# Joining layer norm statistics on GpSimd instead of VectorE in an eight-layer hybrid kernel

## The chip, the cores and the metric

The kernel runs on one core of a Trainium2 chip. The metric is the device time of one execution in microseconds. Before the change it is 443.06 us, the median of 5 runs (441.74 to 447.71). TensorE is called PE, VectorE DVE, ScalarE ACT, GpSimd POOL, and SyncE, which here only issues transfers, SP.

## The reference

The input `x` has 8 sequences of 256 tokens with 128 features, all in float32. Eight layers follow each other. Each reads a layer norm of `x` without weights, and its result is added back to `x`:

```python
x = L0_attn_a_x                      # (8, 256, 128)
x = x + causal_attention(layernorm(x))     # one head, softmax
x = x + ffn_relu(layernorm(x))             # expert 0 of a 128-512-128 network; ends in a layer norm of its own
x = x + linear_attention(layernorm(x))     # no softmax
x = x + ffn_relu(layernorm(x))             # same weights
x = x + retention(layernorm(x))            # 16 heads of 8, decaying causal mask
x = x + ffn_silu(layernorm(x))             # 128-384-128, integer weights times 1/127
x = x + softmax_attention(layernorm(x))    # 16 heads of 8, not causal
x = x + ffn_silu(layernorm(x))             # same weights

def layernorm(x, eps=1e-5):
    m = mean(x, -1); v = var(x, -1)
    return (x - m) / sqrt(v + eps)
```

So there are eight norms ahead of layers and two more inside the two `ffn_relu`.

## The kernel before, in words

The 2048 tokens are cut into four groups of 512 tokens, which are two sequences or four tiles of 128 tokens. A group's `x` stays in SBUF from start to end as a tile of 128 partitions by 4 by 128. Tokens lie on the partitions, so a layer norm's statistics run along the free dimension, one tile of 128x128 at a time.

Each group goes through the layers in order (`layers`, L1341), written as a generator. It asks for a step of an engine with an expected duration (`yield step(DVE, 0.4)`), for buffers (`get`), or for other threads to end (`join`), and then issues the instructions of the step. A planner (`Plan`, L136) runs the four generators and some threads for the weights against each other on a modelled clock while the program is built. Whenever an engine is free, the planner takes the waiting step with the lowest rank. The outcome is one fixed order of instructions on each engine; on the chip each engine then works its list off in that order and waits by semaphores where an operand isn't there.

What the order depends on is: the expected durations in the steps; `RANKS`, one number for each group and layer; `FIRST` and `LAST`, the ranks of the weights' threads; `STALL`, `LEEWAY` and `LATE`, which add to a step's rank or to a buffer's release time; and the times at which the weights' threads start (`plan.start(...)`, L1352 to L1360).

The change is in `layernorm` (L532). For each tile, DVE makes the statistics of the tile with `bn_stats` (L540), which writes six numbers: count, mean and sum of squared deviations of the even elements, and the same for the odd ones. Then DVE joins these to mean and variance with `bn_aggr` (L541). When all tiles are done, four small instructions follow for all tiles at once: variance plus epsilon (L547), minus the mean (L548), the power -1/2 (L551), and the product of minus the mean with it, called `shift` (L552). All four run on POOL. In a quick norm, which only the first layer uses, the first two run on DVE. In all there are 45 calls: 5 quick ones, 32 of four tiles and 8 of two tiles. The last come from the final `ffn_silu`, which works on one sequence at a time.

After that the tiles are normalised by ACT (L558, scale and bias) or DVE (L563, subtract and multiply), whichever the planner finds free. PE transposes them (L579) into PSUM, and ACT or DVE copies them out (L443).

Other names that matter here: in `ffn_relu` (L737) POOL adds the row `b2` to the normalised tiles (L745), `beta` to `x` (L610) and multiplies by `gamma` (L781) after the layer's own norm; its matmuls are L752 and L765. POOL also adds a row to `x` in retention and in softmax attention (L610), sums retention's states (L940) and may take part of its rotation (L831, L837). Preparing weights means the casts of the integer weights on DVE (L509, L510), retention's means (L498, L499) and small products. The softmax attention's scores are L1156, its maxima L1177 on DVE, its exponentials L1211 on ACT, its weighted sums L1228.

Of the kernel before, what the change touches and what calls it, by code (L numbers as in the profile page):

```python
# [30 lines left out]
ALU = mybir.AluOpType  # L31
# [3 lines left out]
B, S, D = 8, 256, 128  # L35
# [10 lines left out]
EPS = 1e-5  # L46
# [21 lines left out]
ARRIVALS = (3.1, 5.1, 6.8, 8.3)  # L68

PAGE, PAGE_US = 256, 3.7  # L70
STALL = 3.87
LEEWAY = 0.04


RANKS = [
    [-4.55, -2.84, -5.08, -11.21, -6.22, 0.79, -0.71, 3.83],
    [0.53, -0.33, -7.21, -3.58, 1.17, -5.41, 2.93, 4.66],
    [2.22, -0.01, -0.03, 8.64, 2.51, 3.26, 3.72, 4.3],
    [3.69, 1.03, 11.09, 5.47, 3.1, 3.24, -6.87, 4.5],
]  # L80
FIRST, LAST = -3.82, 0.45
LATE = 0.55


def of_act(n):
# [217 lines left out]
def step(engine, us, table=None, mode=None, n=None):  # L303

    return ("step", ((engine, us, table),), mode, int(us / 0.053) if n is None else n)
# [23 lines left out]
def hybrid(ctx: ExitStack, tc: tile.TileContext, t: dict, out: bass.AP):  # L329
    nc = tc.nc  # L330
    plan = Plan()
# [96 lines left out]
    def view(buf, pattern, n=N, **sizes):  # L428
        return buf[:, :n].rearrange(pattern, **sizes)

    def flat(tl):
        return tl.rearrange("p a b -> p (a b)")
# [13 lines left out]
    def constants():  # L446
        yield step(POOL, 1.2)
        for e in range(2):
            half = slice(64 * e, 64 * e + 64)
            nc.gpsimd.memset(chunk_mul[half, :], 1.0)  # L450
            nc.gpsimd.affine_select(
                out=chunk_mul[half, :], in_=chunk_mul[half, :], compare_op=ALU.is_ge,
                fill=0.0, base=0, pattern=[[1, 64]], channel_multiplier=-1,
            )
        for store in (r_values, r_spread, l_values, l_spread):
            for _, _, tl in list(store.items):
                if tl.shape[1] == 2:
                    yield step(ACT, of_act(576))
                    nc.scalar.copy(flat(tl), levels[:, 1:2].to_broadcast([P, 2 * tl.shape[2]]))
                else:  # L460
                    for c in range(2):
                        yield step(ACT, of_act(4 * S))
                        nc.scalar.copy(tl[:, :, c, :], levels[:, c : c + 1].unsqueeze(1).to_broadcast([P, 4, S]))
        made["constants"] = True
# [16 lines left out]
    def linear_weights():  # L481

        w = buffer("b_w", [P, P])
        ps = yield get(bank)
        yield step(PE, 0.25)
        nc.tensor.matmul(ps[:, :P], b_tp[:, 1, :], b_tp[:, 0, :], start=True, stop=True)
        yield step(DVE, 0.2)
        nc.vector.tensor_scalar_mul(w, ps[:, :P], float(D**-0.5))
        put(bank, ps)
        made["linear"] = w  # L490
# [41 lines left out]
    def layernorm(src, y, quick=False):  # L532
        s = yield get(small)
        nt = src.shape[1]
        stats = view(s, "p (t c) -> p t c", 6 * nt, t=nt)
        mv = s[:, 24 : 24 + 2 * nt].rearrange("p (t c) -> p t c", t=nt)
        rstd, shift = s[:, 32 : 32 + nt], s[:, 36 : 36 + nt]
        for i in range(nt):
            yield step(DVE, 0.4)
            nc.vector.bn_stats(stats[:, i, :], src[:, i, :])  # L540
            nc.vector.bn_aggr(mv[:, i, :], stats[:, i, :])  # L541
        if quick:
            yield step(DVE, 0.13)
        else:
            yield step(POOL, 1.14 + 0.16 * nt)
        e = nc.vector if quick else nc.gpsimd
        e.tensor_scalar(rstd, mv[:, :, 1], EPS, None, ALU.add)  # L547
        e.tensor_scalar(shift, mv[:, :, 0], -1.0, None, ALU.mult)  # L548
        if quick:
            yield step(POOL, 0.66 + 0.16 * nt)  # L550
        nc.gpsimd.tensor_tensor(rstd, rstd, minus_half[:, :nt], ALU.pow)  # L551
        nc.gpsimd.tensor_tensor(shift, shift, rstd, ALU.mult)  # L552

        def half(tiles):
            for i in tiles:
                e = yield either((ACT, 0.39), (DVE, 0.25), mode=PORT)
                if e == ACT:
                    nc.scalar.activation(  # L558
                        y[:, i, :], src[:, i, :], AF.Identity, bias=shift[:, i : i + 1],
                        scale=rstd[:, i : i + 1],  # L560
                    )
                else:
                    nc.vector.tensor_scalar(  # L563
                        y[:, i, :], src[:, i, :], mv[:, i, 0:1], rstd[:, i : i + 1],
                        ALU.subtract, ALU.mult,
                    )

        yield join([spawn(half(range(k * nt // 2, (k + 1) * nt // 2))) for k in range(2)])
        put(small, s)

# [781 lines left out]
    plan.start(causal_weights(), FIRST, 3.8)  # L1352
    for g in range(GROUPS):
        plan.start(layers(g), g, ARRIVALS[g])
    plan.start(constants(), LAST, 32.4)
    plan.start(linear_weights(), LAST, 15.4)
    plan.start(retention_weights(), LAST, 15.5)
    plan.start(silu_weights(), LAST, 23.7)
    plan.start(softmax_weights(), LAST, 45.7)
    plan.start(pairs_of_scores(), FIRST, 0.0)  # L1360
    plan.run()
    return plan
# [103 lines left out]
```

## Time and profile before

| what | value |
|---|---|
| median of 5 runs | 443.06 us |
| the profiled execution: time, span | 446.1 us, 444.4 us |
| mean granted clock of PE | 0.968 |
| busy: PE | 424.2 us (95%) |
| busy: DVE | 340.2 us (77%) |
| busy: ACT | 233.8 us (53%) |
| busy: POOL | 138.4 us (31%) |
| `bn_stats` on DVE | 160 times, 43.2 us |
| `bn_aggr` on DVE | 160 times, 29.1 us |
| the power on POOL | 45 times, 43.6 us |

A profile is one execution; its span runs from the first to the last instruction, and its time is a little longer than that. The busy shares are averages over stages that have different limits: the first 150 us hold the layers with many norms and small products, and the time from 184 to 398 us holds the softmax attention's scores beside everything else. The chain of waits is followed back from the last instruction; it says what a given stretch was waiting for.

### The profile page before, as it was taken

Reading aid. Unit: us, or ns where it says so; the run is one execution under the profiler, and the core shown is the slowest. Engines: PE = TensorE matmul, PEld = TensorE weight load, DVE = VectorE, ACT = ScalarE, POOL = GpSimd, SP = SyncE. Lnnn points to the kernel's source line nnn. Section 1 sums busy time; section 2 is a strip of 40 time slices with the busy share of each in tenths; the row PEclk is TensorE's granted clock in tenths of the full one; section 3 lists DMA queues with packets and bytes.
Section 4 is the critical chain, followed back from the end, with each engine's and each line's share of the span. In section 5 each row is a group of like instructions: output and inputs, shape, how many; then the busy total and the mean of one; then the engine's idle time right before and its main releaser. Section 6 shows DMA issues by size and latency. Waiting matters only on the chain.

```text
span 444.4 us, 12665 instructions
## 1 busy us (share of the span) xinstructions
PE 424.2 (95%) x5136; PEld 301.7 (68%) x5136; DVE 340.2 (77%) x990; ACT 233.8 (53%) x489; POOL 138.4 (31%) x244
## 2 busy tenths in 40 slices
PE   7899898999996999999999999999999999999996
PEld 6767686675875486767767557766666765674586
DVE  6978998877979879998789989857797615971353
ACT  3589845646152534234567734498416475245642
POOL 4145748859442643021231721301112000020020
PEclk9999999999959999999999999999999999957999
DMA  7300000003000301500001103000200011000001
GB/s 276 124 1 2 1 1 0 1 1 49 3 3 1 50 4 38 62 3 4 4 4 30 25 7 45 3 7 15 37 14 13 15 39 27 3 2 1 1 13 36
DMA packets 8041, 10.73 MB, mean 24 GB/s; under 512 B 1000, under 2 KB 6888, under 8 KB 7984
## 3 DMA queue, kind: packets, MB, share of 16 engines
q1 hardware_dynamic: 7904, 9.81, 9.8%
q8 instruction: 40, 0.66, 0.6%
q14 instruction: 17, 0.14, 0.1%
q10 hardware_dynamic: 80, 0.13, 0.1%
HBM read 4.43 MB, written 1.05 MB: 12 GB/s over the span
## 4 chain that ended last, share of the span: by engine, by line
PE 79%; DVE 13%; POOL 2%; ACT 2%; issue 2%; DMA 1%; DVEq 0%; ACTq 0%; POOLq 0%
PE bank L1156 19%; PE bank L1228 7%; PE bank L1086 5%; PE bank L752 5%; PE bank L1070 5%; PE bank L1076 5%; PE bank L970 4%; PE bank L896 4%; PE bank L765 4%; PE bank L579 2%; PE bank L620 2%; PE bank L817 2%; PE bank L931 2%; DVE small L540 2%; PE bank L1241 2%
## 5 line engine op out<-in xcount | busy, mean ns | idle before, releaser
L1177 DVE TENSOR_REDUCE small<-bank 128x2 f32<-128x512 f32 x128 | 80.4, 681 | 22.3 <-PE bank L1156 21.9
L1211 ACT ACTIVATE probs<-bank 128x512 f32<-128x512 f32 x128 | 68.0, 598 | 44.2 <-PE bank L1156 43.3
L1156 PE MATMUL bank<-l_spread 32*128 32x256 f32 x1024 | 90.8, 418 | 0.0
L547 POOL TENSOR_SCALAR small<-small 128x4 f32<-128x4 f32 (+1 forms) x40 | 11.0, 274 | 215.0 <-DVE small L541 209.9
L1156 PEld LDWEIGHTS bank<-l_spread 32*128 32x128 f32 x1024 | 58.2, 193 | 23.8 <-ACT probs L1211 5.7
L443 ACT COPY work<-bank 128x512 f32<-128x512 f32 (+3 forms) x76 | 35.8, 489 | 58.0 <-PE bank L579 15.3
L558 ACT ACTIVATE work<-x,small 128x128 f32<-128x128 f32 x79 | 34.5, 486 | 30.8 <-POOL small L552 30.8
L551 POOL TENSOR_TENSOR small<-small,mhalf 128x4 f32<-128x4 f32 (+1 forms) x45 | 43.6, 970 | 6.5 <-DVE small L548 6.5
L540 DVE BATCH_NORM_STATS2 small<-x 128x6 f32<-128x128 f32 x128 | 34.6, 270 | 3.6 <-DMA x<-in_x 3.3
L1228 PE MATMUL bank<-probs,l_values 128*32 128x256 f32 x512 | 35.0, 400 | 0.8 <-ACT small L443 0.7
L443 DVE COPY work<-bank 128x256 f32<-128x256 f32 (+3 forms) x36 | 19.0, 530 | 21.0 <-PE bank L1228 16.1
L541 DVE BATCH_NORM_AGGREGATE small<-small 128x2 f32<-128x6 f32 x160 | 29.1, 182 | 5.6
L765 PEld LDWEIGHTS bank<-c_relu,work 128*128 128x128 f32 x256 | 30.2, 192 | 3.2 <-issue 1.6
L765 PE MATMUL bank<-c_relu,work 128*128 128x128 f32 x256 | 32.1, 278 | 0.2 <-DVE work L757 0.2
L752 PE MATMUL bank<-work,c_relu 128*128 128x512 f32 x64 | 31.1, 603 | 1.2 <-ACT work L443 1.0
L579 PE MATMUL bank<-ident,work 128*128 128x128 f32 x128 | 22.8, 292 | 3.3 <-ACT work L558 1.8
L1228 PEld LDWEIGHTS bank<-probs,l_values 128*32 128x32 f32 x512 | 14.3, 112 | 16.6 <-issue 7.4
L1086 PE MATMUL bank<-c_ints,work 128*128 128x128 f32 x192 | 24.8, 279 | 0.0
L940 POOL TENSOR_TENSOR work<-work,work 128x272 f32<-128x272 f32 x16 | 13.0, 817 | 37.9 <-DVE work L918 37.8
L1086 PEld LDWEIGHTS bank<-c_ints,work 128*128 128x128 f32 x192 | 22.9, 192 | 2.6 <-issue 1.5
L1070 PE MATMUL bank<-work,c_ints 128*128 128x256 f32 (+1 forms) x72 | 24.3, 461 | 0.3 <-ACT work L443 0.2
L1076 PE MATMUL bank<-work,c_ints 128*128 128x256 f32 (+1 forms) x72 | 23.0, 453 | 0.0
(155 smaller groups left out, 758.7 us busy)
## 6 DMA issues: line engine op xcount, KB each, us to landing
r_spread<-wide SPq DMA_DIRECT2D x32, 64.0 KB
l_spread<-wide SPq DMA_DIRECT2D x32, 64.0 KB
out<-x SPq DMA_DIRECT2D x8, 128.0 KB
x<-in_x SPq DMA_DIRECT2D x3, 256.0 KB
c_retention_vo<-in_retention_vo SPq DMA_DIRECT2D x1, 713.0 KB
c_relu<-in_relu SPq DMA_DIRECT2D x1, 706.0 KB
c_retention_qk<-in_retention_qk SPq DMA_DIRECT2D x1, 641.0 KB
c_ints<-in_ints SPq DMA_DIRECT2D x1, 576.0 KB
```

Source lines behind the costliest of these rows:

```text
L443: (nc.scalar.copy if e == ACT else nc.vector.tensor_copy)(dst, src)
L540: nc.vector.bn_stats(stats[:, i, :], src[:, i, :])
L551: nc.gpsimd.tensor_tensor(rstd, rstd, minus_half[:, :nt], ALU.pow)
L752: nc.tensor.matmul(ps, w1[:, c * P : (c + 1) * P], yT[:, :N], start=True, stop=True)
L765: nc.tensor.matmul(ps[:, n * D : (n + 1) * D], h[c][:, i * P : (i + 1) * P], w2[:, c, :], start=(c == 0), stop=(c == 3),)
L1070: nc.tensor.matmul(ps[:, :n], w_gate[:, cols], yT[:, :n], start=True, stop=True)
L1076: nc.tensor.matmul(ps[:, :n], w_up[:, cols], yT[:, :n], start=True, stop=True)
L1086: nc.tensor.matmul(ps[:, (i - first) * D : (i - first + 1) * D], h[c][:, i * P : (i + 1) * P], w_down[:, c, :], start=(c == 0), stop=(c == 2),
L1156: nc.tensor.matmul(to[k][:, n * S : (n + 1) * S], seq.spread[rows, j, of_keys, n * P : (n + 1) * P], seq.spread[rows, j, 1 - of_keys, :], ...
L1177: nc.vector.tensor_reduce(nmax[:, h2 % 4 // 2, 2 * (h2 % 2) + k, :], ps[k].rearrange("p (m s) -> p m s", m=2), AX.X, ALU.max, negate=True,)
L1211: nc.scalar.activation(p[:, k, :], ps[k], AF.Exp)
L1228: nc.tensor.matmul(o[32 * i : 32 * (i + 1), (j % 2) * S : (j % 2 + 1) * S], seq.v[:, c, VONE * h : VONE * h + 32], seq.p[h2][0][:, k, c * ...
```

## The change

For all norms but the quick ones, `bn_aggr` is left out. POOL instead takes the six numbers of each tile and joins even and odd halves for all tiles at once: it multiplies means and sums by -1/2, subtracts one half's mean from the other's, adds the halves (which gives minus the mean, and minus half the sum of squares), squares the difference, scales the sum of squares to a variance plus epsilon, adds the squared difference, takes the power and multiplies. That is eight POOL instructions where there were four. DVE's application reads `rstd` and `shift` now, and multiplies and adds, where it read the mean and `rstd`. The expected durations in the steps are set to match: 0.21 in place of 0.4 for DVE by tile, and 2.15 in place of 1.14 plus 0.16 by tile for POOL. The ranks, the other constants of the planner and the start times of the weights' threads have new values.

```diff
-STALL = 3.87
-LEEWAY = 0.04
+STALL = 2.03
+LEEWAY = 0.03
 RANKS = [
-    [-4.55, -2.84, -5.08, -11.21, -6.22, 0.79, -0.71, 3.83],
-    [0.53, -0.33, -7.21, -3.58, 1.17, -5.41, 2.93, 4.66],
-    [2.22, -0.01, -0.03, 8.64, 2.51, 3.26, 3.72, 4.3],
-    [3.69, 1.03, 11.09, 5.47, 3.1, 3.24, -6.87, 4.5],
+    [-2.47, -1, -0.56, -0.78, 0.53, -0.85, -3.55, 4.76],
+    [1.17, 1.49, -1.96, 2.09, 0.91, -0.95, 0.29, 4.49],
+    [1.18, 3.27, 2.95, 2.48, 1.61, 2.16, -1.27, 4.8],
+    [2.62, 5.15, 10.69, 5.72, 4.27, 2.04, -1.62, 3],
 ]
-FIRST, LAST = -3.82, 0.45
-LATE = 0.55
+FIRST, LAST = -1.34, 4.23
+LATE = 1.22
...
-        stats = view(s, "p (t c) -> p t c", 6 * nt, t=nt)
-        mv = s[:, 24 : 24 + 2 * nt].rearrange("p (t c) -> p t c", t=nt)
+        stats = view(s, "p (t k c) -> p t k c", 6 * nt, t=nt, k=2)
+        sums = s[:, 24 : 24 + 2 * nt].rearrange("p (t c) -> p t c", t=nt)
         rstd, shift = s[:, 32 : 32 + nt], s[:, 36 : 36 + nt]
         for i in range(nt):
-            yield step(DVE, 0.4)
-            nc.vector.bn_stats(stats[:, i, :], src[:, i, :])
-            nc.vector.bn_aggr(mv[:, i, :], stats[:, i, :])
+            yield step(DVE, 0.4 if quick else 0.21)
+            nc.vector.bn_stats(flat(stats[:, i]), src[:, i, :])
+            if quick:
+                nc.vector.bn_aggr(sums[:, i, :], flat(stats[:, i]))
         if quick:
             yield step(DVE, 0.13)
+            nc.vector.tensor_scalar(rstd, sums[:, :, 1], EPS, None, ALU.add)
+            nc.vector.tensor_scalar(shift, sums[:, :, 0], -1.0, None, ALU.mult)
+            yield step(POOL, 0.66 + 0.16 * nt)
+            nc.gpsimd.tensor_tensor(rstd, rstd, minus_half[:, :nt], ALU.pow)
+            nc.gpsimd.tensor_tensor(shift, shift, rstd, ALU.mult)
         else:
-            yield step(POOL, 1.14 + 0.16 * nt)
-        e = nc.vector if quick else nc.gpsimd
-        e.tensor_scalar(rstd, mv[:, :, 1], EPS, None, ALU.add)
-        e.tensor_scalar(shift, mv[:, :, 0], -1.0, None, ALU.mult)
-        if quick:
-            yield step(POOL, 0.66 + 0.16 * nt)
-        nc.gpsimd.tensor_tensor(rstd, rstd, minus_half[:, :nt], ALU.pow)
-        nc.gpsimd.tensor_tensor(shift, shift, rstd, ALU.mult)
+
+            yield step(POOL, 2.15 + 0.16 * nt)
+            halves, mean = stats[:, :, :, 1:], sums[:, :, 0]
+            nc.gpsimd.tensor_scalar(halves, halves, -0.5, None, ALU.mult)
+            nc.gpsimd.tensor_tensor(rstd, halves[:, :, 0, 0], halves[:, :, 1, 0], ALU.subtract)
+            nc.gpsimd.tensor_tensor(sums, halves[:, :, 0, :], halves[:, :, 1, :], ALU.add)
+            nc.gpsimd.tensor_tensor(rstd, rstd, rstd, ALU.mult)
+            nc.gpsimd.tensor_scalar(sums[:, :, 1], sums[:, :, 1], -2.0 / D, EPS, ALU.mult, ALU.add)
+            nc.gpsimd.tensor_tensor(rstd, rstd, sums[:, :, 1], ALU.add)
+            nc.gpsimd.tensor_tensor(rstd, rstd, minus_half[:, :nt], ALU.pow)
+            nc.gpsimd.tensor_tensor(shift, mean, rstd, ALU.mult)
...
                     nc.vector.tensor_scalar(
-                        y[:, i, :], src[:, i, :], mv[:, i, 0:1], rstd[:, i : i + 1],
-                        ALU.subtract, ALU.mult,
+                        y[:, i, :], src[:, i, :], rstd[:, i : i + 1], shift[:, i : i + 1],
+                        ALU.mult, ALU.add,
                     )
...
-    plan.start(constants(), LAST, 32.4)
-    plan.start(linear_weights(), LAST, 15.4)
-    plan.start(retention_weights(), LAST, 15.5)
-    plan.start(silu_weights(), LAST, 23.7)
-    plan.start(softmax_weights(), LAST, 45.7)
+    plan.start(constants(), LAST, 29.2)
+    plan.start(linear_weights(), LAST, 28)
+    plan.start(retention_weights(), LAST, 29.7)
+    plan.start(silu_weights(), LAST, 27.2)
+    plan.start(softmax_weights(), LAST, 37.2)
```

## The prediction

> **What bounds the kernel now.** I read the page's busy shares first, then the windows cut at the places where GpSimd's load changes, then the chain of waits around 67 us, then GpSimd's timeline there, and last the groups by line.
>
> ```profile
> span 444.4 us, 12665 instructions
> PE 424.2 (95%) x5136; PEld 301.7 (68%) x5136; DVE 340.2 (77%) x990; ACT 233.8 (53%) x489; POOL 138.4 (31%) x244
> ```
>
> TensorE (PE) is idle for only 444.4 - 424.2 = 20.2 us. VectorE (DVE), which the change relieves, is second at 77%; GpSimd (POOL), which it loads, has 31%. Averages decide nothing, so by stretch (columns: window, its length, then the busy time of PE, PE's loads, DVE, ACT and POOL, the granted clock):
>
> ```profile
> 20.00:67.00 47.00, 45.12 (x291) 35.23 (x289) 41.34 (x150) 35.92 (x81) 24.55 (x44) 1.00 0.01 2
> 67.00:93.20 26.20, 24.56 (x142) 17.63 (x142) 20.40 (x70) 16.41 (x35) 23.10 (x37) 1.00 0.00 1
> ...
> 100.90:113.50 12.60, 12.60 (x121) 8.39 (x120) 9.99 (x30) 7.28 (x13) 12.12 (x17) 1.00 0.30 44
> 113.50:150.00 36.50, 31.52 (x576) 24.41 (x574) 32.68 (x105) 13.27 (x30) 13.11 (x24) 0.86 0.08 14
> 150.00:380.00 230.00, 227.62 (x3409) 155.53 (x3408) 182.16 (x471) 122.65 (x249) 50.63 (x85) 1.00 0.11 20
> ```
>
> From 150 to 380 us PE is idle for 230.00 - 227.62 = 2.4 us: nothing taken from DVE there can show. From 20 to 67 us it is idle for 1.9 us, from 67 to 93 for 1.6. POOL, at 31% overall, has 23.1 of 26.2 us in the feed-forward stretch from 67 to 93 and 12.1 of 12.6 from 101 to 113. The chain of waits (start, length, engine, line) passes through it:
>
> ```profile
> 66.75 0.19 DVE small L541
> 66.95 0.08 issue
> 67.02 0.23 POOL small L547
> 67.26 0.08 issue
> 67.34 0.23 POOL small L548
> 67.56 1.00 POOL small L551
> 68.57 0.04 issue
> 68.65 0.20 POOL small L552
> 68.85 1.23 POOL work L745
> 70.07 1.23 POOL x L610
> 71.30 1.24 POOL work L781
> ```
>
> The reader sees one layer norm's four POOL instructions (67.02 to 68.85: 1.83 us) and three additions of rows queued right behind them, all on the path.
>
> **The change, part by part.** *Removed from DVE.* Every layer norm but the 16 tiles of the quick ones loses its bn_aggr: 160 - 16 = 144.
>
> ```profile
> L541 DVE BATCH_NORM_AGGREGATE small<-small 128x2 f32<-128x6 f32 x160 | 29.1, 182 | 5.6
> L547 POOL TENSOR_SCALAR small<-small 128x4 f32<-128x4 f32 x32 | 8.8, 274 | 103.1 <-DVE small L541 98.1 <-DVE small L679 4.3
> L552 POOL TENSOR_TENSOR small<-small 128x4 f32<-128x4 f32 x35 | 7.0, 201 | 2.8
> L803 DVE TENSOR_TENSOR small<-small 128x32 f32<-128x32 f32 x24 | 4.6, 192 | 0.8
> ```
>
> On the chain a bn_aggr holds 0.18 us and 0.02 of issue: 0.20. DVE is relieved of 144 x 0.20 = 28.8 us. On the chain that ended last I count 41 of them in all: 28 between 22 and 67 us, 4 at 73 to 75, 5 at 143 to 146, 4 at 187 to 189. So the chain holds 8.2 us of it. But the gain can't exceed PE's idle time beside it: of the 28 x 0.20 = 5.6 us before 67 us, at most 1.9 come back, since PE works in the rest. I take -1.9.
>
> *Added on POOL.* Four instructions become eight: two tensor_scalar, the power and the last product stay, four small tensor_tensor are new, in 40 layer norms. A tensor_tensor of 128x4 takes 0.20 (L552). The lower bound is 0.20 x 4 = 0.8 us a norm. The upper bound takes the gap between two such instructions where one waits for the other: L547 to L548 starts 0.31 to 0.32 us apart, so 4 x 0.31 = 1.24. About half of the new ones wait for the instruction ahead, so I take 1.0, and 40 us over the kernel. A norm of 4 tiles thus gets 1.0 - 4 x 0.20 = 0.2 us longer from first statistic to last product; a norm of 2 tiles 1.0 - 0.4 = 0.6.
>
> *What is queued behind it on POOL.* 20 to 67 us: 8 norms add 8 us to 24.6 of 47; it fits, and the norm's own 0.2 is inside the noise. 67 to 93.2: 7 norms add 7.0 us where POOL's idle time is 26.2 - 23.1 = 3.1, and most of that is the 0.08 us between its own dependent instructions; only the 0.66 ahead of one norm can be used.
>
> ```profile
> 72.61 0.73 POOL L547 TENSOR_SCALAR small<-small 128x4 f32<-128x4 f32 x1
> ...
> 75.07 0.23 POOL L547 TENSOR_SCALAR small<-small 128x4 f32<-128x4 f32 x1
> ...
> 77.56 0.23 POOL L547 TENSOR_SCALAR small<-small 128x4 f32<-128x4 f32 x1 [0.66 <-DVE small L541]
> ```
>
> By the end of this run the queue is 7.0 - 0.7 = 6.3 us late, at this order. How much reaches PE? Zero, if it always has another group's work; 6.3, if it has none. The first three norms (67.0, 72.6, 75.1) stand in one POOL queue that is itself the chain up to 76.9: 3 x 1.0 = 3.0 us, and DVE's four bn_aggr saved at 73 to 75 save nothing as the POOL queue is the later one. The other four stand beside a chain on PE; of their 3.3 I take half. Together +4.6. From 100.9 to 113.5 two norms add 2.0 us with nothing free; behind them are the row additions and the sums of states (L940) that retention's weighted products wait for. PE is at 12.60 of 12.60 there and idle by 0.7 just after, so between 0 and 2.0: +1.0. What is late next is the transposes (L579) of those groups, and with them their first matmuls.
>
> *The norms at 145 and 189 us* are on the chain: -5 x 0.20 + 1.0 = 0, and -4 x 0.20 + 1.0 = +0.2. *The tail:* the norm of two tiles at 427.4 releases the last transposes on PE at 430.4, so its 0.6 counts: +0.6.
>
> *A new wait for DVE.* The application on DVE (L563) now reads shift, the last product, where it read the mean and the power's result: 0.20 + 0.07 later (L552 and its gap). DVE waited for the power twice (2.0 us); 2 x 0.27 = +0.5.
>
> *Moved for nothing.* The weights' preparation starts later (linear 15.4 to 28, retention 15.5 to 29.7, the casts of the integer weights 23.7 to 27.2; softmax and the constants earlier). The casts L509/L510 now lie on the chain at 24.6 to 26.2; that is in the capped 1.9 us already. Their first readers are the linear layer at some 68 us, retention at some 87, the gated feed-forward at 150, so DVE's slack covers them; without it, the casts' 1.6 us would come back on the path. The same DMAs are issued.
>
> *The order.* New ranks put every queue into another order, which this trace can't show. Its cost lies between taking away all of PE's idle time from 20 to 150 us (1.9 + 1.6 + 0.8 + 5.0 = 9.3 us) together with a stretch of low clock, and adding such a stretch:
>
> ```profile
> 124.00:126.00 2.00, 2.00 (x78) 2.00 (x79) 1.76 (x8) 1.65 (x4) 1.76 (x5) 0.50 0.00 0
> ...
> 390.00:406.00 16.00, 16.00 (x110) 9.83 (x109) 6.90 (x17) 6.94 (x14) 2.67 (x8) 0.50 0.01 2
> ```
>
> The clock is at half from 122.6 to 132.9 and from 389 to 406 us: 5.1 and 8.5 us lost. I take 0 for the order, and keep -14 and +8.5 for the range.
>
> **The sum.** -1.9 + 4.6 + 1.0 + 0.0 + 0.2 + 0.6 + 0.5 = +5.0 us. The profiled execution took 446.1 us (span 444.4 and 1.7 around it), so the changed kernel's like would take 451.1; the median of the five runs is 443.06, and on that scale it is 448.1.
>
> Two rules of the Trainium skill, which the sum does without. Row: at 128 x 4 a POOL tensor_tensor takes 201 ns (L552), a DVE one at 128 x 32 takes 192. "GPSIMD Engine Reference", section 4.1, speaks against the change: elementwise work belongs on VectorE, being about twice as slow on GPSIMD for two inputs. By that the four would cost some 4 x 0.38 = 1.5 us a norm and the sum would be about +8; at this size the rows don't show the factor. Row: the clock was halved at 122.6 us after a stretch in which PE was busy for 3.3 of 4 us, and stayed whole after 138 to 142 us, with PE busy for 1.4 of 4. "TensorE: Matmul & The Clock Gate", Part 1, has the clock halved after an idle window of some 3.4 us; the rows bear that out only in part, and by the rule alone no added gap of mine, all under 3 us, would cost a stretch.
>
> **The rivals.** *A: DVE was the brake, faster.* For it: DVE is busy for 41.3 of 47 us from 20 to 67, and the chain holds 8.2 us of bn_aggr. If the new order spreads the norms so that POOL has over 2 us free between two of them in the feed-forward stretch, its additions vanish in the 69% that it is idle, and the relief counts fully on a PE whose idle time of 9.3 us before 150 us it can fill: -8.2 + 0.2 + 0.6 + 0.5 = -6.9, 436.2 us. Against: 5.6 of those 8.2 stand where PE has 1.9 to give. *B: nothing shows.* PE has 95%; the lateness hides in other groups' work, and gain and loss are both under 2 us: -1.9 + 0.2 + 0.6 + 0.5 = -0.6, 442.5. Against: the chain's 7 us on POOL at 67 to 77. *C: the lateness starves PE into a third low-clock stretch*: 448.1 + 5.1 = 453.2. *D: the change does not relieve DVE*, as POOL and DVE hold each other up: L547 takes 0.73 at 72.61 instead of 0.23. Forty such delays of 0.5 give 20 us on POOL, and a fifth of them on the path 4 us: 452, inside C's range.
>
> **How the numbers follow.** My forecast (POOL's queue is late) has 0.40, C and D together 0.10, B 0.18, A 0.32. The predicted time is the forecast's, 448.1; its own range is 444.5 to 452. For eight in ten the range must take in A and C: 436.2 and 453.2, and a little of the order's bounds on both sides: 435.5 to 456. A measurement of this kernel tells about 1%, 4.4 us, from no change. Slower by more than that is the forecast's upper part with C and D, 0.48; faster is A with the order's gains, 0.32; within it are B and the forecast's low end, 0.20.
>
> **What would show it.** Right: L541 falls to 16, DVE's busy time by 26 to 29 us, POOL's rises to some 175, and POOL is full in the feed-forward stretch, with waits of ACT (L558) on the last product above the present 31.4 us; PE's idle time before 115 us grows. Wrong: PE's idle time before 150 us falls below 9 us, or ACT's wait for POOL shrinks; then DVE was the brake. A low-clock loss other than 13.6 us is the order's doing and neither.

## The result and the profile after

The changed kernel takes 439.88 us in the median (437.74 to 445.46, 46 runs), the kernel before 443.49 us (437.59 to 453.61, 86 runs, those beside the experiments included). The ratio of the two is 0.9966, with a 95% interval of 0.9948 to 0.9983: 0.34%, or 1.5 us, less. The prediction said 5.0 us more. The sign was wrong; the time lies inside the range. Here and below a ratio counts only executions within 1.5% of the fastest of the same kernel on the same chip, so it can differ from that of two medians (which lie 0.8% apart here).

The profiled execution after took 438.1 us at a mean granted clock of 0.996, where the one before had 446.1 us at 0.968. Its head, and the shares of its chain of waits by engine:

```profile
span 436.3 us, 12698 instructions
PE 415.1 (95%) x5136; PEld 292.3 (67%) x5136; DVE 319.2 (73%) x842; ACT 237.7 (54%) x495; POOL 170.5 (39%) x402
...
PE 76%; POOL 10%; DVE 9%; issue 2%; DMA 1%; ACT 1%; SPq 0%; POOLq 0%; DVEq 0%
```

VectorE lost 21.0 us of busy time and GpSimd gained 32.1. The idle time of TensorE is what it was: 436.3 - 415.1 = 21.2 us, where it was 20.2. So the shorter span of this one execution is shorter busy time of TensorE for the same 5136 matmuls, in line with its higher clock, and not idle time won back. By stretch (window, length, busy time of PE, its loads, DVE, ACT, POOL, then clock):

```profile
20.00:67.00 47.00, 45.50 (x287) 34.95 (x286) 39.22 (x122) 36.61 (x80) 31.71 (x81) 1.00 0.01 2
67.00:93.20 26.20, 23.37 (x150) 17.80 (x149) 12.82 (x36) 13.39 (x30) 21.98 (x47) 1.00 0.00 1
93.20:113.50 20.30, 15.55 (x60) 8.84 (x59) 15.36 (x39) 11.06 (x21) 18.10 (x35) 0.92 0.16 24
113.50:150.00 36.50, 36.48 (x886) 28.98 (x888) 31.95 (x90) 13.03 (x30) 20.48 (x42) 1.00 0.15 20
150.00:380.00 230.00, 226.21 (x3217) 152.77 (x3210) 176.65 (x425) 126.78 (x259) 65.02 (x154) 1.00 0.11 19
```

From 20 to 150 us TensorE is idle for 1.5 + 2.8 + 4.75 + 0.0 = 9.1 us; before it was 1.9 + 1.6 + 0.8 + 5.0 = 9.3. The idle time moved from the last stretch to the two ahead of it. From 67 to 93 us GpSimd is the fullest engine after TensorE, from 93 to 113 us it is the fullest of all, and the chain of waits shows how it holds the others up. One norm of four tiles, and the start of the next, in the chain of the changed kernel (start, length, engine, tile, line):

```profile
50.34 0.47 DVE small L540 x2
50.81 0.08 issue
50.89 0.27 POOL small L554
51.16 0.07 issue
51.23 0.20 POOL small L555
51.44 0.15 POOL small L556
51.59 0.17 POOL small L557
51.76 0.07 issue
51.83 0.21 POOL small L558
52.04 0.07 issue
52.11 0.21 POOL small L559
52.33 0.07 issue
52.39 1.05 POOL small L560
53.44 0.07 issue
53.51 0.20 POOL small L561
53.71 0.08 issue
53.80 0.36 POOL small L554
```

From 50.89 to 53.71 this norm takes 2.82 us where the one shown before took 1.83: +0.99 us, as forecast (1.0). The gap of 0.07 us stands ahead of L555, L559, L560 and L561, which read what the instruction before them wrote, and ahead of L558, which reads what L556 wrote; L556 and L557, which also don't read the one just ahead, follow it without a gap. Behind this norm come two more, straight after each other, so that the third waits for two that have nothing to do with it. The waits of the changed kernel (who waits, for whom: us in total, times, longest):

```profile
ACT work L567 <- POOL small L561: 43.7, 29, 7.5
...
DVE work L572 <- POOL small L561: 13.7, 12, 2.6
```

ScalarE's waits for `shift` (now L561) went from 31.4 to 43.7 us, and VectorE's, which had been for the power, from 2.0 to 13.7. And `bn_aggr` is down to the 16 quick tiles:

```profile
L542 DVE BATCH_NORM_AGGREGATE small<-small 128x2 f32<-128x6 f32 x16 | 2.9, 182 | 0.6
```

These are signs that the prediction gave for its own mechanism, yet the time went the other way. So the experiments take apart what the diff does at once: VectorE's relief, GpSimd's load, and the new order.

### The profile page after: what moved, and what is told of

The parts are those of the page before. It is cut to its first block, busy times and chain, and to the rows that moved or that the text cites. A ratio compares the mean times of both kernels' runs of the same rounds, so it can differ in the third digit from the quotient of the medians.

```text
span 436.3 us, 12698 instructions
## 1 busy us (share of the span) xinstructions
PE 415.1 (95%) x5136; PEld 292.3 (67%) x5136; DVE 319.2 (73%) x842; ACT 237.7 (54%) x495; POOL 170.5 (39%) x402
## 4 chain that ended last, share of the span: by engine, by line
PE 76%; POOL 10%; DVE 9%; issue 2%; DMA 1%; ACT 1%; SPq 0%; POOLq 0%; DVEq 0%
PE bank L1165 18%; PE bank L1237 7%; PE bank L1095 5%; PE bank L1079 4%; PE bank L1085 4%; PE bank L905 4%; PE bank L774 3%; POOL small L560 3%; PE bank L979 3%; PE bank L761 3%; PE bank L629 2%; PE bank L940 2%; PE bank L588 2%; PE bank L1250 2%; PE bank L868 2%
## 5 line engine op out<-in xcount | busy, mean ns | idle before, releaser
L1165 PE MATMUL bank<-l_spread 32*128 32x256 f32 x1024 | 84.5, 400 | 0.0
L554 POOL TENSOR_SCALAR small<-small 128x16 f32<-128x16 f32 (+1 forms) x40 | 12.4, 310 | 183.8 <-DVE small L540 164.0
L1165 PEld LDWEIGHTS bank<-l_spread 32*128 32x128 f32 x1024 | 52.8, 184 | 23.0 <-issue 10.4
L443 ACT COPY work<-bank 128x512 f32<-128x512 f32 (+3 forms) x82 | 38.9, 485 | 47.1 <-PE bank L588 15.3
L560 POOL TENSOR_TENSOR small<-small,mhalf 128x4 f32<-128x4 f32 (+1 forms) x40 | 39.3, 983 | 3.1
L540 DVE BATCH_NORM_STATS2 small<-x 128x6 f32<-128x128 f32 x128 | 29.4, 277 | 3.8 <-DMA x<-in_x 3.5
L588 PE MATMUL bank<-ident,work 128*128 128x128 f32 x128 | 23.1, 289 | 6.2 <-ACT work L567 5.4
L443 DVE COPY work<-bank 128x512 f32<-128x512 f32 (+3 forms) x30 | 15.8, 542 | 14.7 <-PE bank L1326 5.8
L588 PEld LDWEIGHTS bank<-ident,work 128*128 128x128 f32 x128 | 15.2, 144 | 15.9 <-ACT work L567 9.0
L1081 ACT ACTIVATE work<-bank 128x256 f32<-128x256 f32 (+1 forms) x36 | 15.7, 454 | 15.7 <-PE bank L1079 15.2
L624 DVE TENSOR_TENSOR x<-bank,x 128x256 f32<-128x256 f32 (+1 forms) x36 | 15.9, 448 | 10.7 <-PE bank L1095 5.6
```

What stands on the lines that cost most here:

```text
L443: (nc.scalar.copy if e == ACT else nc.vector.tensor_copy)(dst, src)
L588: nc.tensor.transpose(ps[:, i * P : (i + 1) * P], y[:, i, :], ident)
L1165: nc.tensor.matmul(to[k][:, n * S : (n + 1) * S], seq.spread[rows, j, of_keys, n * P : (n + 1) * P], seq.spread[rows, j, 1 - of_keys, :], ...
```

## The experiments

### The norm and the order, each alone

The planner makes an order from the expected durations and the ranks, not from the instructions. So the instructions of the norm can be exchanged at a fixed order: one leaves the durations in the steps as they were. The first kernel is the kernel before with only the norm's instructions changed; the second is the changed kernel with the old norm's.

```diff
# e1: kernel before, its steps and ranks kept
             yield step(DVE, 0.4)
-            nc.vector.bn_stats(stats[:, i, :], src[:, i, :])
-            nc.vector.bn_aggr(mv[:, i, :], stats[:, i, :])
+            nc.vector.bn_stats(flat(stats[:, i]), src[:, i, :])
...
             yield step(POOL, 1.14 + 0.16 * nt)
+            (the eight instructions of the change)
```

> The join alone: every queue keeps the order of the kernel before, and only the norms' instructions are those after the change (no bn_aggr, eight POOL instructions, the application on VectorE reads shift). Theory Q (POOL's queue is late at a given order, as forecast; the new ranks gave it back): 4 to 6 us slower than before, by the forecast's sum of +5.0. Theory H (the join is hidden and the ranks do nothing): within 1.5 us of before. Theory D (VectorE was the brake; the relief pays and the new ranks lose some of it): 4 to 7 us faster.

> The ranks alone: every queue has the order after the change, and the norms' instructions are those before it (bn_aggr on VectorE by tile, four POOL instructions). The changed kernel is 1.5 us faster than before. Theory Q: about 5 us faster than the changed kernel, so 6 us faster than before. Theory H: as the changed kernel, 1 to 2 us faster than before. Theory D: 4 us or more slower than before.

Measured: the new norm in the old order takes 453.33 us, ratio 1.0318 (1.0257 to 1.0378), 14 us more. The old norm in the new order takes 445.97 us, ratio 1.0087 (1.0044 to 1.0130). Neither half alone is a gain. The order alone is a small loss, the norm alone a large one, and together they are slightly faster: each order suits its own norm. Where the 14 us arise is seen on TensorE's own milestones at the same order, the first and the last start of two groups of matmuls (durations min/median/max in ns, then first and last start). So there are four milestones; the third is where TensorE enters the softmax attention. Before:

```profile
L717 PE MATMUL bank<-work x32: 273/275/368, 54.7 to 133.7; 128*128 128x128 f32 x32
...
L1156 PE MATMUL bank<-l_spread x1024: 374/374/791, 183.2 to 418.6; 32*128 32x256 f32 x171
```

and the new norm in the old order:

```profile
L726 PE MATMUL bank<-work x32: 275/275/417, 59.1 to 142.6; 128*128 128x128 f32 x32
...
L1165 PE MATMUL bank<-l_spread x1024: 374/374/792, 194.2 to 424.5; 32*128 32x256 f32 x171
```

It is late by 4.4 us at 55 us, by 8.9 at 134 and by 11.0 at 183. Low clock up to these three starts costs 1.6, 3.4 and 6.8 us here, and 0, 5.1 and 5.1 in the profile before, so it is part of the first and of the third. Little more is lost in the attention behind (it is late by 5.9 at its end, at 419 us, but the profile before lost 8.5 us there to a stretch of half clock from 389 to 406 us, and this one 1.7). The chain of waits of this kernel at the place where the first 4.4 us arise:

```profile
46.53 0.77 POOL small L554
...
48.53 1.05 POOL small L560
...
49.93 0.36 POOL small L554
...
52.63 0.21 POOL small L561
52.84 0.03 issue
52.87 2.50 DVE work L572 x2
55.36 0.05 issue
55.41 0.55 PE bank L588 x3
55.95 3.33 PE bank L761 x4
```

Two norms stand behind each other on GpSimd from 46.5 to 52.8 us; then two normalisations on VectorE (L572), the transposes and the feed-forward's matmuls wait. In the chain of the kernel before the same two normalisations are

```profile
49.99 2.59 DVE work L563 x2
```

as long, and 2.9 us earlier. So the stretch that the prediction costed at nothing ("it fits") is the one where the lateness begins. The rest of the 4.4 us is the clock: it is 0.58 from 56 to 60 us in this execution, 1.7 us lost.

### The relief alone and the load alone

Both keep the order before. The first takes `bn_aggr` away and puts nothing on GpSimd: mean and variance of the even half of the features are used, and the odd half is left out. The second keeps `bn_aggr` and adds four dependent instructions on GpSimd, whose result nobody reads.

```diff
# e3
-            nc.vector.bn_aggr(mv[:, i, :], stats[:, i, :])
+            if quick:
+                nc.vector.bn_aggr(mv[:, i, :], stats[:, i, :])
...
+        if not quick:
+            mv = stats[:, :, 1:3]
# e4
+        if not quick:
+            more = s[:, 40 : 40 + nt]
+            nc.gpsimd.tensor_tensor(more, mv[:, :, 0], mv[:, :, 1], ALU.subtract)
+            nc.gpsimd.tensor_tensor(more, more, mv[:, :, 0], ALU.add)
+            nc.gpsimd.tensor_tensor(more, more, more, ALU.mult)
+            nc.gpsimd.tensor_tensor(more, more, mv[:, :, 1], ALU.add)
```

> Order of before; bn_aggr is left out of all but the quick norms and nothing joins the halves: the four POOL instructions take the even half's statistics, so the odd half is left out of the computation. It measures the relief of VectorE by itself (28.8 us of its time). Theory Q: the gain is capped by TensorE's idle time beside it, 1 to 3 us faster. Theory H: within 1 us. Theory D: 6 to 8 us faster, the 41 bn_aggr on the chain at 0.20 us.

> Order of before; bn_aggr stays on VectorE and four more small POOL instructions of the joins' size, each waiting for the one ahead, stand ahead of the old four in every norm but the quick ones; their result is not used. It measures the load on POOL by itself, without the relief (some 1.1 us a norm). Theory Q: 7 to 9 us slower (4.6 in the feed-forward stretch, 1.0 after it, 1.0 for each norm on the chain at 145, 189 and 427 us). Theory H: within 1.5 us. Theory D: within 2 us.

Measured: the relief alone 440.43 us, ratio 0.9954 (0.9914 to 0.9995), some 2.0 us less; the load alone 459.76 us, ratio 1.0430 (1.0382 to 1.0478), some 19 us more. With the load alone TensorE's first milestone is at 58.4 us and its third at 198.2, 15.0 us late, of which 3.4 is lower clock on the way (8.5 us lost against 5.1). With the relief alone they are

```profile
L720 PE MATMUL bank<-work x32: 272/275/275, 55.3 to 132.3; 128*128 128x128 f32 x32
...
L1159 PE MATMUL bank<-l_spread x1024: 374/374/478, 183.3 to 411.4; 32*128 32x256 f32 x171
```

that is, TensorE enters the attention at 183.3 us, as before at 183.2, though VectorE has 21.9 us less to do. (Low clock cost 6.8 us up to there, against 5.1, so at equal clock it would be some 2 us earlier.) The two effects together, +19 and -2, give +17 where both at once gave +14. The relief was right in the prediction (-1.9). The load was not: one microsecond a norm costs much more than the 4.6 and 1.0 us that the sum had for GpSimd's queue.

### The ranks by themselves

Here the steps carry the durations of the norm that is in the kernel, but the ranks, the constants and the start times of the weights' threads are those of the other kernel.

```diff
# e5: the changed kernel with the old values; e6: the kernel before with the new ones
-STALL = 2.03
+STALL = 3.87
...
-    [-2.47, -1, -0.56, -0.78, 0.53, -0.85, -3.55, 4.76],
+    [-4.55, -2.84, -5.08, -11.21, -6.22, 0.79, -0.71, 3.83],
...
-    plan.start(linear_weights(), LAST, 28)
+    plan.start(linear_weights(), LAST, 15.4)
```

> The changed kernel with the ranks, the other constants and the start times of before; the expected durations in the steps are those after the change, so the planner knows that a norm holds POOL for about 1 us longer and makes its own order for it. The join in the unchanged order took 12 us more than before, the changed kernel 1.5 us less. Theory S (the planner's knowledge of the durations gave the 12 us back): within 3 us of the changed kernel. Theory R (the search for ranks gave it back): 6 us or more slower than before.

> The kernel before with the ranks, constants and start times after the change; its own norms and its own durations. Theory T (ranks are good for one set of durations only): 4 us or more slower than before, as the old norms in the new kernel's order were. Theory U (the new ranks are better ones in themselves, and hide a loss of the join): 4 us or more faster than before.

Measured: the new norm with the old ranks 459.10 us, ratio 1.0303 (1.0173 to 1.0432, a wide interval). The old norm with the new ranks 482.91 us, ratio 1.0913 (1.0838 to 1.0988). Ranks are thus no property of the network that could be moved from one norm to the other: with steps shorter or longer by 0.2 and 1.0 us they make another order, and a bad one. Telling the planner the right durations didn't help either: e5 has them and is no better than e1, which lies to it. What gave the 14 us back is the set of ranks found for these durations.

### What the join costs in the new order, and a shorter norm on GpSimd in the old

The first kernel is the changed one, its order kept, with neither `bn_aggr` nor the join (the odd half of the features is left out again). The second has the old norm and order, but the first two of the four small instructions on VectorE, after the last `bn_aggr`, so that GpSimd has two a norm.

```diff
# e8: the changed kernel, its steps and ranks kept
             yield step(POOL, 2.15 + 0.16 * nt)
-            (the eight instructions of the change)
+            sums = stats[:, :, 0, 1:]
+            nc.gpsimd.tensor_scalar(rstd, sums[:, :, 1], EPS, None, ALU.add)
+            nc.gpsimd.tensor_scalar(shift, sums[:, :, 0], -1.0, None, ALU.mult)
+            nc.gpsimd.tensor_tensor(rstd, rstd, minus_half[:, :nt], ALU.pow)
+            nc.gpsimd.tensor_tensor(shift, shift, rstd, ALU.mult)
# e7: the kernel before
-        e = nc.vector if quick else nc.gpsimd
-        e.tensor_scalar(rstd, mv[:, :, 1], EPS, None, ALU.add)
-        e.tensor_scalar(shift, mv[:, :, 0], -1.0, None, ALU.mult)
+        nc.vector.tensor_scalar(rstd, mv[:, :, 1], EPS, None, ALU.add)
+        nc.vector.tensor_scalar(shift, mv[:, :, 0], -1.0, None, ALU.mult)
```

> Order of the changed kernel; neither bn_aggr nor the joins: four POOL instructions on the even half's statistics, so the odd half is left out of the computation. POOL is relieved of 1.1 us a norm. Theory Q: POOL still sets the pace from 50 to 100 us, 5 us or more faster than the changed kernel. Theory P (the new order has made room for the joins): within 2 us of the changed kernel.

> The kernel before with its order on every queue, but the two small tensor_scalar of every norm (variance plus epsilon, minus the mean) run on VectorE right after the last bn_aggr instead of on POOL: POOL is relieved of some 0.6 us a norm, VectorE gets some 0.2 to 0.3. Theory Q (POOL's time in a norm reaches the end at a given order; 1.1 us of it cost 15 us or more): 3 to 6 us faster than before. Theory H (POOL's time in a norm is at the knee: longer costs, shorter gives nothing since TensorE is full): within 1.5 us.

Measured: without the join the new order takes 432.96 us, ratio 0.9814 (0.9749 to 0.9879) to the kernel before. GpSimd leaves the chain of waits, which holds in this kernel

```profile
PE 91%; DVE 5%; ACT 2%; issue 1%; DMA 1%; DVEq 0%
```

and the milestones stand, without it and with it (the changed kernel), at the same order and the same mean clock of 0.996, at

```profile
L722 PE MATMUL bank<-work x32: 275/275/275, 55.7 to 133.3; 128*128 128x128 f32 x32
...
L1161 PE MATMUL bank<-l_spread x1024: 374/374/478, 182.2 to 408.4; 32*128 32x256 f32 x171
```

```profile
L726 PE MATMUL bank<-work x32: 275/275/275, 55.7 to 138.6; 128*128 128x128 f32 x32
...
L1165 PE MATMUL bank<-l_spread x1024: 374/374/478, 187.5 to 414.4; 32*128 32x256 f32 x171
```

No lateness at the first milestone, 5.3 us at the second and the third, 6.0 at the end. The new order hides the join up to 56 us, which is where the old one lost its first 4.4, and pays for it once, between 56 and 139 us. All ratios to the kernel before, by order and norm:

| order | no join, no `bn_aggr` | `bn_aggr` on VectorE | join on GpSimd |
|---|---|---|---|
| of the kernel before | 0.9954 | 1 | 1.0318 |
| of the changed kernel | 0.9814 | 1.0087 | 0.9966 |

Read along the rows: `bn_aggr` costs 0.46% in the old order and 2.7% in the new; the join costs 3.6% (16 us) in the old and 1.5% (6.7 us) in the new. The same work has a price that differs with the order, by a factor of two and more; how much more is not settled for `bn_aggr`, as the 0.46% has an interval of 0.05 to 0.86.

The kernel with two instructions on VectorE takes 444.84 us, ratio 1.0045 (1.0005 to 1.0086). GpSimd's busy time fell from 138.4 to 120.6 us and that gave nothing, while VectorE's rise from 340.2 to 349.4 cost a little. So the old order showed no gain for a shorter norm on GpSimd, and a large loss for a longer one (+19 us for the load alone). That looks like a knee rather than a slope, but it isn't shown: this kernel moves work instead of removing it, and VectorE's rise may hide a gain.

### Both norms with ranks searched for them

The comparison of the two kernels is one of two norms, each with the ranks somebody found for it. So I searched again: ranks, constants and start times varied at random, kept where the end on the planner's own clock became earlier, which is a choice among orders and no time of the chip. The old norm:

```diff
-    [-4.55, -2.84, -5.08, -11.21, -6.22, 0.79, -0.71, 3.83],
+    [-40.467, -94.884, -15.209, -53.779, -49.83, -35.621, -24.579, 22.452],
... (three more rows of RANKS, STALL, LEEWAY, FIRST, LAST, LATE)
-    plan.start(linear_weights(), LAST, 15.4)
+    plan.start(linear_weights(), LAST, 39.674)
... (four more start times)
```

> The kernel before, its norms and durations unchanged, with another set of ranks, constants and start times, found by a further search from its own. Theory V (what the changed kernel gained is what any fresh set of ranks gains or loses; the join adds nothing): 1 to 4 us faster than before, so at least as fast as the changed kernel. Theory W (the old norms' order was spent, the join opened room): within 2 us of before, or slower.

Measured: 437.24 us (436.36 to 438.65), ratio 0.9888 (0.9848 to 0.9929). The old norm beats both kernels when its ranks are searched again. The new norm, with 2.3 in place of 2.15 in GpSimd's step:

> The changed kernel with a norm's expected duration on POOL raised by 0.15 us, to the 2.9 to 3.0 us that its profile shows, and ranks searched further for that. Theory Q (POOL's queue is what its order underrates): 1 to 3 us faster than the changed kernel, 3 to 5 faster than before. Theory V: within 3 us of the changed kernel on either side, as any fresh set of ranks.

Measured: 454.87 us, ratio 1.0288 (1.0243 to 1.0332). In this set one start time is plainly wrong. The search had put the preparation of the gated feed-forward's weights at 9.5 us, as if the data had landed by then, but on the chip VectorE stood still for it (waits from 0 to 45 us):

```profile
DVE c_ints L509 <- DMA c_ints<-in_ints: 3.9, 1, 3.9
```

That is 3.9 of some 13 us that this kernel is slower; the rest isn't explained. So the search was repeated with the start times of the linear layer's, retention's and the gated feed-forward's weights no lower than the lowest that the two kernels have, once with 2.3 in GpSimd's step and once with the changed kernel's own durations.

```diff
# e13; e14 keeps 2.15 and has other ranks
-            yield step(POOL, 2.15 + 0.16 * nt)
+            yield step(POOL, 2.3 + 0.16 * nt)
... (RANKS, the other constants and the start times, as found)
```

> The changed kernel's norms, a norm's expected duration on POOL 0.15 us longer, ranks searched further with no weights' thread ahead of its data. Theory V (an order is as good as its search, the norm's form matters little): within 3 us of the changed kernel, up to 5 us faster than before. Theory X (the join's POOL time is dear in any order): slower than the old norms with searched ranks, which took 437.2 us, by 4 us or more.

> The changed kernel, its own expected durations, ranks searched further from its own. Theory V: 1 to 4 us faster than the changed kernel, as the old norms gained 5 us from a further search. Theory X: within 2 us of the changed kernel or slower, as the planner still underrates POOL.

Measured: 447.67 us, ratio 1.0113 (1.0056 to 1.0169), and 442.14 us, ratio 1.0003 (0.9961 to 1.0045). With five sets of ranks the join thus stands at -0.3, 0.0, +1.1, +2.9 (the set with the wrong start time) and +3.0%, and the old norm with three at -1.1, 0 and +9.1%. The +3.0 and the +9.1 are those with ranks found for the other norm. The gain of 0.34% is smaller than the scatter from the choice of ranks alone. That the join can't be brought to -1.1% isn't shown: four searches are no proof.

### A third norm: each element counted twice

If `bn_aggr` is to go without a load on GpSimd, the statistics of the whole row have to come out of `bn_stats` itself. It reads the elements by turns into an even and an odd half. Where each element is read twice in a row, through a view that repeats it, the even half is the whole row; then the four old instructions do, with the even half's sum of squares scaled by 1/D.

```diff
-            nc.vector.bn_stats(stats[:, i, :], src[:, i, :])
-            nc.vector.bn_aggr(mv[:, i, :], stats[:, i, :])
+                twice = src[:, i, :].unsqueeze(2).to_broadcast([P, D, 2])
+                nc.vector.bn_stats(stats[:, i, :], twice)
...
-        e.tensor_scalar(rstd, mv[:, :, 1], EPS, None, ALU.add)
+            mv = stats[:, :, 1:3]
+            nc.gpsimd.tensor_scalar(rstd, mv[:, :, 1], 1.0 / D, EPS, ALU.mult, ALU.add)
```

First in the order before, then with two sets of searched ranks (in the second the softmax weights' preparation starts at 36.4 us, in the first at 15.4):

> The same norms as the kernel with doubled statistics, but with the order of the kernel before on every queue: VectorE gets 0.13 us a tile more and is relieved of 0.20, POOL is as before. Theory Q: between the kernel without bn_aggr or join (0.5% faster than before) and before, some 0.5 to 1 us faster than before. Theory D (VectorE's relief pays): 2 us or more faster.

> Neither bn_aggr nor the joins, with the whole statistics: bn_stats reads every element twice (a broadcast view of 128x2), so that the even half is the whole row; it costs VectorE some 0.13 us a tile more than the plain one where bn_aggr cost 0.20; POOL keeps four instructions, with the first one scaling as well. Ranks are searched for these durations from the changed kernel's. Theory Q (both VectorE and POOL pay at the order's knee, so taking from both is the gain): 4 to 8 us faster than before, 3 to 6 faster than the changed kernel. Theory V (an order is as good as its search): within 3 us of the changed kernel.

> Doubled statistics, neither bn_aggr nor joins, ranks searched further from those that gave 0.5% below before, with no weights' thread ahead of its data. Theory V: as that run, 0 to 1% below before. Theory X (with both VectorE and POOL relieved an order finds more room): below the old norms with searched ranks, 1.2% or more below before.

Measured: 441.55 us, ratio 0.9988 (0.9945 to 1.0032) in the old order; 440.10 us, 0.9950 (0.9918 to 0.9982) and 438.49 us, 0.9886 (0.9827 to 0.9944) with searched ranks. The group of the doubled statistics in the first of them:

```profile
L545 DVE BATCH_NORM_STATS2 small<-x 128x6 f32<-128x256 f32 x112 | 40.7, 413 | 0.2
L541 DVE BATCH_NORM_STATS2 small<-x 128x6 f32<-128x128 f32 x16 | 4.4, 275 | 3.9 <-DMA x<-in_x 3.9
```

413 ns where the plain one of the quick norms takes 275: 0.138 us more a tile, in place of the 0.20 that `bn_aggr` holds on the chain. It takes a little from VectorE (336.9 us busy against 340.2), puts nothing on GpSimd, and with the second set of searched ranks beats both kernels, though by no more than the old norm with searched ranks. With the first set it beats the kernel before alone. It can't be said from these runs which of those two is the better norm.

## Why the prediction was wrong

**The order: "I take 0".** This is the step that failed and that turned the sign. The bounds beside it (-14 to +8.5, low clock included) were right to be wide, but the value between them was taken as if the old order stayed. At the old order the change costs 3.2% (e1). The new one brings that to -0.3%: 15.5 us back, at the bound of -14 within what e1's interval leaves open (2.7 us either way). Some 6 us of it goes with less low clock (median loss 11.1 us in e1, 3.5 in the changed kernel; the account is below), the rest with the order itself. The old norm gains nothing from the new order (e2, +0.9%), so it isn't a better order, only one made for these durations. What it does is visible in two places: in it the join makes the first milestone no later, where it cost 4.4 us in the old order (1.6 of it low clock), and TensorE is busy for 36.48 of 36.50 us from 113.5 to 150, where it lacked 5.0.

**The load on GpSimd: the size of two terms.** The price of one norm was right: 0.99 us against 1.0. GpSimd's busy time came to 170.5 us against "some 175". But "8 norms add 8 us to 24.6 of 47; it fits" was wrong at the order it was made for: 4.4 us late at the first milestone. Idle time summed over a stretch doesn't say that it lies where the queue needs it; the chain showed two norms back to back with VectorE's work waiting behind them. In all, the sum had +5.0 us at the old order and the chip had +14 (+9.6 at equal clock, by the account below). The later stretches make up most of the rest (+8.9 at 134 us, +11.0 at 183 us). The sum also passed over 0.84 us in which GpSimd stood idle at 85 us, and the estimate with 1.5 us a norm comes to +9.5, not to +8; neither changes the outcome.

**VectorE's relief.** -1.9 us was forecast from TensorE's idle time, and the relief alone gave some 2.0 (e3, 0.2 to 3.8). The cap fits that, and rival A, with 6.9 us of gain, was wrong at the old order. In the new order the relief is worth 2.7% (old norm against none, 1.0087 to 0.9814), 12 us (7.6 at equal clock): a cap read from one order's idle time doesn't hold for another's.

**The rivals.** B named nearly the right time (442.5), but not for its reason: much of the 32 us added on GpSimd was hidden, but not down to 2 us, since GpSimd is 10% of the chain of the changed kernel and taking the join away saves 6.7 us. D, that the two engines hold each other up, has something to it: the first small instruction takes 0.77 us instead of 0.27 where it stands beside VectorE's work in e1, and two normalisations on VectorE take 1.25 us each (their group's mean is 0.41) where GpSimd adds 128x512 tiles. But the same two take 2.59 us together in the kernel before as well, so there it is no cost of the change. What it costs in total wasn't measured by itself. C, a third stretch of low clock, didn't occur in the profiled execution of the changed kernel, whose clock of 0.996 is the highest that its 46 show (the lowest is 0.979).

**What was to show it.** `bn_aggr` at 16, ScalarE's wait for `shift` above 31.4 us (43.7), TensorE's idle time before 115 us (4.3 to 9.1 from 20 to 113.5): as forecast. From 67 to 93 us GpSimd was busy for 22.0 us, no more than before (23.1); it became fuller on both sides of that stretch. VectorE's busy time fell by 21.0 rather than 26 to 29: `bn_aggr` itself went by 26.2 us, but other instructions were busy for longer. The new order isn't the reason, since the fall is 21.9 in the old one too (e3). The sign that would have spoken for A, less than 9 us idle before 150 us, stayed out by a hair (9.1). The signs were those of a mechanism, and most came out right while the time did not, because none of them asked whether the new order makes up for it.

**The clock.** The measured gain is about as large as the difference in low clock. Each run gives the granted clock and the span, hence the time lost, (1 - clock) x span: in the median 7.0 us for the kernel before and 3.5 for the changed one. Over the runs of one kernel the time rises by 0.78 us (before, 80 runs) to 0.88 (after, 46 runs) for each microsecond lost. Taking off 0.8 of each run's loss leaves 436.1 us before and 437.0 after: no gain at equal clock, rather a loss of about 1 us. So the measured sign hangs on low clock, while 8.7 of the 9.6 us that the change costs in the old order (445.7 in e1) are won back at equal clock. By the same account the join costs 11.5 us in the old order and 5.9 in the new, `bn_aggr` 1.9 and 7.6; the old norm with searched ranks has 435.4 and the doubled statistics, with the second set, 432.4. The two profiled executions agree: the changed kernel enters the softmax attention at 187.5 us, 4.3 us later than the kernel before, and is ahead at its end (414.4 against 418.6 us) by less than the 8.5 us that the kernel before loses to half clock at 389 us. That the new order causes the smaller loss wasn't shown; no experiment set the clock.

## What to carry to other kernels

Where an order is searched for, change the instructions first at a fixed order, by keeping the durations that the planner is told, and only then search, for both sides and equally long; otherwise the comparison is one of two searches. An engine's microsecond has no price of its own: here the same join cost 16 us in one order and 6.7 in another (11.5 and 5.9 at equal clock), so idle time added up over a stretch is no proof that new work fits. Where an engine is to be relieved, look whether its own instruction can do more (a repeated view) before the work goes to another engine's queue.

## What the runs showed of the hardware

The clock was whole or half in all 17 profiles, and stretches at half had 10.2 and 17.1 us before and 3.4 us after. By the traces' records of the granted clock, all 54 stretches at half that end within a span last 3.4 us or a whole multiple of it (up to 27.3), and within one profile they start whole multiples of 3.4 us apart. The one of the changed kernel lies behind a stretch in which TensorE was idle or nearly so (windows of 2 us; PE busy, its loads, DVE, ACT, POOL, then clock):

```profile
100.00:102.00 2.00, 0.00 (x0) 0.00 (x0) 2.00 (x5) 0.53 (x2) 1.88 (x3) 1.00 0.00 0
102.00:104.00 2.00, 1.04 (x4) 0.48 (x4) 2.00 (x3) 1.58 (x5) 1.92 (x2) 1.00 0.01 4
104.00:106.00 2.00, 1.40 (x2) 0.64 (x3) 1.72 (x3) 0.55 (x1) 1.83 (x5) 0.71 0.00 0
106.00:108.00 2.00, 2.00 (x4) 0.70 (x3) 0.22 (x1) 0.23 (x1) 1.76 (x5) 0.50 0.09 33
```

TensorE's longest gap ahead of it, in brackets, is 2.90 us:

```profile
102.45 0.33 PE L588 MATMUL bank<-ident,work 128*128 128x128 f32 x1 [2.90 <-ACT work L567]
```

That is less than an idle window of some 3.4 us, after which the Trainium skill, "TensorE: Matmul & The Clock Gate", Part 1, has the clock halved. In all profiles only two of the 54 stretches stand close behind a gap of 3.4 us or more (in e6 and e11), and the stretch at 122.6 us in the profile before came after TensorE had been busy for 3.3 of 4 us, which the rule does not explain. What starts a stretch, and why the loss varies from run to run of one kernel, stays open.

A `bn_stats` over a view that reads each of 128 elements twice takes 413 ns against 275: half again as long for twice the reads. And at 128x4 a GpSimd instruction takes 0.20 us, of which 0.15 to 0.17 remain as its pace where the next one doesn't read its result, and 0.27 to 0.28 (0.20 and a gap of 0.07) where it does. One instruction, L558, has the gap without reading the one ahead, which these runs don't explain.
